# Adapter factors gathered per sequence and packed two to a pass, with weight rounding interleaved, in a one-core transformer block

## The chip, the cores and the metric

The kernel runs on one core of one Trainium2 chip. The metric is the device time of one execution, in microseconds, as the median of several runs. The profile comes from one further execution of the same program, taken by the hardware profiler.

## The reference

A batch `x` of 16 sequences of 128 tokens, 256 wide, in f32, goes through one block. A first attention conditions `x`; a gated delta-rule attention over it is added to `x`. What follows is the stage that the change is about:

```python
x = x + attn(cond(x, ...), ...)                     # call it x1
Ai, Bi = A[adapter_indices], B[adapter_indices]     # one of 8 adapters of rank 16 for each sequence
lora_linear(x, W, A, B) = x @ W + (x @ Ai) @ Bi
gate = lora_linear(x1, Wg, Ag, Bg)                  # 256 -> 1024
up   = lora_linear(x1, Wu, Au, Bu)
y    = lora_linear(silu(gate) * up, Wd, Ad, Bd)     # 1024 -> 256
qm(x, w, scale) = (x @ w.astype(float8_e4m3fn).astype(x.dtype)) * scale
x  = x1 + qm(silu(qm(y, gate_w)) * qm(y, up_w), down_w)     # 256 -> 768 -> 256
```

So each sequence needs only its own adapter, and the three weights of the last feed-forward part are first rounded to the values that an 8-bit float can hold.

## The kernel before, in words

The 16 sequences form four groups of four (`GS` = 4 sequences, `GT` = 512 tokens). The first two attentions take some 2040 us: 64 units (a key head and a group) go through a software pipeline whose steps have due times inside a slot; `plan` writes them down and a sort orders them. The scheduler of the language then settles the order of the instructions on each engine, and adds the waits. The last 420 us are the feed-forward stage, from line 875. Between the two, tiles of the new stage are placed over the memory of the old ones, so a first write there waits for whatever used that memory last.

**The seam.** `project` (L765) adds up each group's attention output in PSUM over the 16 units (L771). On the last unit VectorE adds `x` to it (L776) and SyncE's queue stores the result in the HBM buffer `x1` (L777). It does so in two halves; they share one buffer `x_in`, and the second half of `x` is loaded (L779, `load_x`) when the first half has been stored. `ffn_loads` (L787), called two slots after the last unit began, loads the adapters' first factors `ag`, `au`, the weights `wg`, `wu` and the second factors `bg`, `bu` into memory that the attention no longer uses.

**The feed-forward stage.** All of `x1` is loaded into `acc` (L886), then the other weights. The first and second factors of all 8 adapters stand side by side: 8 adapters x 16 ranks = 128 columns. The kernel computes all 128 ranks for every token and zeroes those of the other adapters: `onehot` (L908) has a one where a row belongs to a sequence's adapter, and `masked` (L928) multiplies with it on VectorE.

`adapted(g)` makes the steps of a group: two `turn`s (TensorE transposes, L941, and a ScalarE copy to `x1T`, L942), two `low`s (L947, one for gate and one for up), eight `hidden(i)`, then `low_down` (L969) and two `down`s (L978 and, for the adapter, L979). A `hidden` step computes 128 of the 1024 hidden columns: two matmuls with the weight (L955) and one with the second factor (L956) for the gate, SiLU on ScalarE (L962), the same three matmuls for up, and the product on VectorE (L964). `quantized(g)` is the 8-bit part: `fuse` (L997, L999, L1002, L1003) and `down` (L1011, VectorE's scale L1015, GpSimd's addition of `acc` L1016, the store L1017). `merge` interleaves the steps of `adapted(g)` with those of `quantized(g - 1)` evenly, by their place in their own lists; group 0's `adapted` runs alone.

**Rounding.** `quantize` (L911) rounds a weight in place. VectorE masks the exponent and scales it (L913, L914), adds and subtracts it (L915, L916); GpSimd checks for overflow in four instructions (L917 to L920). It is called for `gq`, `uq` and `dq` ahead of group 0's steps, and the three share one scratch buffer `qm`, so that each begins when GpSimd has finished the one before.

Of the kernel before, what the change touches and what calls it, by code (L numbers as in the profile page):

```python
# [8 lines left out]
F32 = mybir.dt.float32  # L9
# [6 lines left out]
P = 128  # L16
NB = 16
# [23 lines left out]
NAD = 8  # L41
QI = 768
# [11 lines left out]
def tile_adaln_attn_ffn(  # L54
# [4 lines left out]
    wg, wu, wd, ag, bg, au, bu, ad, bd,  # L59
# [47 lines left out]

    beta = keep.tile([P, NK, NB, 2], F32, name="beta")
# [6 lines left out]
    onehot = keep.tile([P, NB], F32, name="onehot")  # L115
# [267 lines left out]
    def load_o(u):  # L383
        kh, g = u
        wo = w_o[u] = late["w"].tile([P, 2, D], F32, name="wo_head", tag="wo")
        nc.sync.dma_start(out=wo, in_=w_out[kh * 2 * P : (kh + 1) * 2 * P, :].rearrange("(h p) e -> p h e", p=P))
        if kh == NK - 1:
            load_x(g, 0)

    def load_x(g, n):  # L390
        x_in[g, n] = late["p"].tile([P, 2, D], F32, name="x_in", tag="x_in")
        b0 = g * GS + 2 * n
        nc.sync.dma_start(out=x_in[g, n], in_=x[b0 : b0 + 2].rearrange("b s d -> s b d"))
# [359 lines left out]
    def finish_unit(u):  # L753

        kh, g = u
        d = un[u]

        def turn(n):
            ps = ps_b.tile([P, 4, S], F32, name="ps_zt", tag="b")
            for j in range(4):  # L760
                T.transpose(ps[:, j, :], d["z"][:, 4 * n + j, :], ident)  # L761
            d["zT", n] = late["p"].tile([P, 4, S], F32, name="zT", tag="zT", bufs=2)
            A.activation(d["zT", n], ps, AF.Copy, scale=nw)  # L763

        def project(n):  # L765
            if kh == 0:
                x_in[g, "ps", n] = ps_r.tile([P, 2, D], F32, name="ps_out", tag="r")
            ps = x_in[g, "ps", n]
            for j in range(2):
                for h in range(2):  # L770
                    T.matmul(ps[:, j, :], lhsT=d["zT", n][:, 2 * j + h, :], rhs=w_o[u][:, h, :],  # L771
                             start=kh == j == h == 0, stop=kh == NK - 1 and j == h == 1)
            if kh == NK - 1:
                part = x_in[g, n]
                b0 = g * GS + 2 * n
                V.tensor_tensor(part, ps, part, ALU.add)  # L776
                nc.sync.dma_start(out=x1[b0 : b0 + 2].rearrange("b s d -> s b d"), in_=part)  # L777
                if n == 0:
                    load_x(g, 1)  # L779
            if n == 1:  # L780
                del un[u]

        return [lambda: turn(0), lambda: turn(1), lambda: project(0), lambda: project(1)]
# [3 lines left out]
    def ffn_loads():  # L787
        def loaded(name, src, tag, **kw):
            t = pre[name] = pa.tile([P, FI], F32, name=name, tag=tag, **kw)
            nc.sync.dma_start(out=t, in_=src)  # L790

        low = pa.tile([P, 2, ND, P], F32, name="low_sb", tag="prod")
        for i, (name, src) in enumerate((("ag", ag), ("au", au))):
            pre[name] = low[:, i]
            nc.sync.dma_start(out=low[:, i], in_=src.rearrange("(c p) r -> p c r", p=P))
        loaded("wg0", wg[0:P], "kq", bufs=2)
        loaded("wg1", wg[P:D], "kq", bufs=2)
        loaded("bg", bg, "sqa")
        loaded("wu0", wu[0:P], "lanes")
        loaded("wu1", wu[P:D], "inv")  # L800
        loaded("bu", bu, "diag")
# [73 lines left out]
    with ExitStack() as st:  # L875
        w3 = st.enter_context(tc.tile_pool(name="w3", bufs=1))
        p3 = st.enter_context(tc.tile_pool(name="p3", bufs=2))
        ps_g = st.enter_context(tc.tile_pool(name="ps_g", bufs=4, space=PSUM))
        ps_x = st.enter_context(tc.tile_pool(name="ps_x", bufs=4, space=PSUM))
# [6 lines left out]
        acc = w3.tile([P, NB, D], F32, name="acc3", tag="acc3")  # L886
        for g in range(NG):
            nc.sync.dma_start(out=acc[:, g * GS : (g + 1) * GS, :], in_=x1[g * GS : (g + 1) * GS].rearrange("b s d -> s b d"))
        tok = loaded([P, NB], itok.partition_broadcast(P), "tok", I32)
# [3 lines left out]
        ad_sb = loaded([P, NFI, P], ad.rearrange("(c p) r -> p c r", p=P), "ad_sb")  # L893
        wd_sb = loaded([P, NFI, D], wd.rearrange("(c p) e -> p c e", p=P), "wd_sb")
        bd_sb = loaded([P, D], bd, "bd_sb")
# [5 lines left out]
        tokf = w3.tile([P, NB], F32, name="tokf")  # L901
        V.tensor_copy(tokf, tok)
        row_16 = w3.tile([P, 1], I32, name="row_16")
        G.iota(row_16, pattern=[[0, 1]], base=0, channel_multiplier=1)
        V.tensor_scalar(row_16, row_16, 4, None, ALU.arith_shift_right)
        rowf_16 = w3.tile([P, 1], F32, name="rowf_16")
        V.tensor_copy(rowf_16, row_16)
        V.tensor_scalar(onehot, tokf, rowf_16, None, ALU.is_equal)  # L908


        def quantize(t, n):  # L911
            m = w3.tile([P, QI * ND], F32, name="qm", tag="qm")[:, :n]
            V.tensor_scalar(m.bitcast(I32), t.bitcast(I32), 0x7F800000, None, ALU.bitwise_and)  # L913
            V.tensor_scalar(m, m, 2.0**-6, 1.5 * 2.0**20, ALU.max, ALU.mult)  # L914
            V.tensor_tensor(t, t, m, ALU.add)  # L915
            V.tensor_tensor(t, t, m, ALU.subtract)  # L916
            G.tensor_tensor(m, t, t, ALU.mult)  # L917
            G.tensor_scalar(m, m, 448.0 * 448.0, 3e38, ALU.is_gt, ALU.mult)
            G.tensor_scalar(m, m, 3e38, 0.0, ALU.mult, ALU.mult)
            G.tensor_tensor(t, t, m, ALU.add)  # L920

        quantize(gq.rearrange("p c f -> p (c f)"), ND * QI)
        quantize(uq.rearrange("p c f -> p (c f)"), ND * QI)
        quantize(dq.rearrange("p c e -> p (c e)"), NQI * D)
# [3 lines left out]
        def masked(dst, ps, g):  # L928
            V.tensor_tensor(dst.rearrange("p (s t) -> p s t", t=S), ps.rearrange("p (s t) -> p s t", t=S),
                            onehot[:, g * GS : (g + 1) * GS][:, :, None].to_broadcast([P, GS, S]), ALU.mult)  # L930

        def adapted(g):
            d = grp3[g] = {}

            def turn(c):
# [4 lines left out]
                for s in range(GS):  # L940
                    T.transpose(ps[:, s, :], acc[:, g * GS + s, c * P : (c + 1) * P], ident)  # L941
                A.copy(d["x"][:, c, :], ps.rearrange("p s t -> p (s t)"))  # L942

            def low(name, w):
                ps = ps_x.tile([P, GT], F32, name="ps_low", tag="x")
                for c in range(ND):
                    T.matmul(ps, lhsT=w[:, c, :], rhs=d["x"][:, c, :], start=c == 0, stop=c == ND - 1)  # L947
                d[name] = p3.tile([P, GT], F32, name=name, tag=name)
                masked(d[name], ps, g)

            def one_of(w, b, low_name, i):
                ps = ps_g.tile([P, GT], F32, name="ps_gu", tag="g")
                cols = slice(i * P, (i + 1) * P)
                for c in range(ND):
                    T.matmul(ps, lhsT=pre[f"{w}{c}"][:, cols], rhs=d["x"][:, c, :], start=c == 0, stop=False)  # L955
                T.matmul(ps, lhsT=b[:, cols], rhs=d[low_name], start=False, stop=True)  # L956
                return ps

            def hidden(i):
                pg = one_of("wg", pre["bg"], "lg", i)  # L960
                gs = p3.tile([P, GT], F32, name="gs", tag="gs")
                A.activation(gs, pg, AF.Silu)  # L962
                pu = one_of("wu", pre["bu"], "lu", i)
                V.tensor_tensor(d["h"][:, i, :], pu, gs, ALU.mult)  # L964

            def low_down():
                ps = ps_x.tile([P, GT], F32, name="ps_ld", tag="x")
                for i in range(NFI):
                    T.matmul(ps, lhsT=ad_sb[:, i, :], rhs=d["h"][:, i, :], start=i == 0, stop=i == NFI - 1)  # L969
                d["ld"] = p3.tile([P, GT], F32, name="ld", tag="ld")  # L970
                masked(d["ld"], ps, g)
                d["y"] = p3.tile([P, ND, GT], F32, name="yT", tag="yT")

            def down(e):
# [4 lines left out]
                T.matmul(ps, lhsT=bd_sb[:, cols], rhs=d["ld"], start=False, stop=True)  # L979
# [3 lines left out]
                [lambda: turn(0), lambda: turn(1), lambda: low("lg", pre["ag"]), lambda: low("lu", pre["au"])]  # L983
# [4 lines left out]
        def quantized(g):  # L988
# [17 lines left out]
            def down(n):  # L1006
# [9 lines left out]
                G.tensor_tensor(o, o, acc[:, b0 : b0 + 2, :], ALU.add)  # L1016
                nc.sync.dma_start(out=out[b0 : b0 + 2].rearrange("b s d -> s b d"), in_=o)  # L1017

            return [lambda i=i: fuse(i) for i in range(NQI)] + [lambda: down(0), lambda: down(1)]

        for g in range(NG + 1):
# [3 lines left out]
            if g:  # L1025
                lists.append(quantized(g - 1))
            merge(*lists)
# [8 lines left out]
def _layouts(i):  # L1036
# [4 lines left out]
    adapters = lambda a: c(np.asarray(a).transpose(1, 0, 2).reshape(a.shape[1], -1))  # L1041
    rows = lambda a: c(np.asarray(a).reshape(-1, a.shape[2]))
# [22 lines left out]
        "ag": adapters(i["L0_cond2_Ag"]),  # L1065
        "bg": rows(i["L0_cond2_Bg"]),
        "au": adapters(i["L0_cond2_Au"]),
        "bu": rows(i["L0_cond2_Bu"]),
        "ad": adapters(i["L0_cond2_Ad"]),
        "bd": rows(i["L0_cond2_Bd"]),  # L1070
# [23 lines left out]
```

## Time and profile before

| | us |
|---|---|
| median of 3 runs | 2471.11 (2468.83 to 2472.75) |
| the profiled execution's own time | 2466.78 |
| its span, first to last instruction | 2465.1 |
| last attention matmul L771 begins | 2039.05 |
| first matmul of the feed-forward stage begins | 2050.27 |
| product L964 that ended TensorE's longest wait in this stage begins | 2093.96 |
| L979 of group 0 begins | 2123.16 |
| last matmul L1011 begins its 10.52 us | 2449.03 |

How it is read: the page gives one execution on the slowest core, here the only one. The first part of the page is:

```profile
span 2465.1 us, 41929 instructions
PE 2233.8 (91%) x16264; PEld 1479.0 (60%) x16264; DVE 1548.6 (63%) x2099; ACT 1357.5 (55%) x3004; POOL 1123.0 (46%) x813
```

PE is TensorE's matmuls, PEld its weight loads, DVE VectorE, ACT ScalarE, POOL GpSimd. SP is SyncE, which here issues DMAs; "SPq" is its queue. The page's second part cuts the span into 40 equal slices of 61.6 us, with the busy share in tenths. In a timeline a row has the start, the length, the engine, the line, and out<-in with shapes; equal instructions that follow each other are merged, with x for their number, and in brackets stands how long the engine was idle ahead of the row and what ended that. A logical f32 matmul is two records. A row's length includes the time until the last result is out, so the distance between two starts is the better measure of what a row occupies.

### The profile page before, as it was taken

How to read it: one execution, taken by the hardware profiler on the slowest of the kernel's cores; microseconds unless marked ns; L12 is line 12 of the kernel's file. 1: busy time of each engine (PE TensorE's matmuls, PEld its weight loads, DVE VectorE, ACT ScalarE, POOL GpSimd, SP SyncE). 2: the span in 40 equal slices, each digit the busy share in tenths (PEclk: the TensorE clock that was granted, in tenths of full speed). 3: DMA queues.
4: the chain of work that ended last, by engine and by line, in shares of the span. 5: the costliest groups of instructions: out<-in, count | busy, mean ns of one | idle time of the engine just before them, and what ended most of it. 6: DMA issues, size and time to landing. Idle time of an engine off the chain costs nothing. (4 is left out here: it accounts for less than half of the span.)

```text
span 2465.1 us, 41929 instructions
## 1 busy us (share of the span) xinstructions
PE 2233.8 (91%) x16264; PEld 1479.0 (60%) x16264; DVE 1548.6 (63%) x2099; ACT 1357.5 (55%) x3004; POOL 1123.0 (46%) x813
## 2 busy tenths in 40 slices
PE   7868768999999899999989899998999996999999
PEld 3434336666767676676667666766767783444545
DVE  4657888777686967768696877769686523111111
ACT  4665546766767676667667666666766660111010
POOL 4685526555564656455564655556463214200000
PEclk9889879999999999999999999999999998999999
DMA  1200122222323222223223222233223213000000
GB/s 59 96 7 23 27 63 58 76 67 67 80 77 80 78 76 63 72 70 83 80 79 77 68 68 68 70 86 84 72 63 82 71 32 115 0 5 5 9 1 17
DMA packets 290580, 146.13 MB, mean 59 GB/s; under 512 B 184016, under 2 KB 279376, under 8 KB 290384
## 3 DMA queue, kind: packets, MB, share of 16 engines
q1 hardware_dynamic: 289952, 143.41, 21.5%
q8 instruction: 131, 2.15, 0.4%
q14 instruction: 65, 0.53, 0.1%
q10 hardware_dynamic: 432, 0.04, 0.0%
HBM read 116.91 MB, written 5.51 MB: 50 GB/s over the span
## 5 line engine op out<-in xcount | busy, mean ns | idle before, releaser
L437 DVE SCALAR_TENSOR_TENSOR cv<-ps_in,cw,cv 128x508 f32<-128x508 f32 (+2 forms) x768 | 541.1, 738 | 88.1 <-ACT cv L435 83.4
L426 PE MATMUL ps_in<-hT,w_v 128*128 128x512 f32 x512 | 280.7, 677 | 6.9 <-DVE z L741 4.6
L435 ACT ACTIVATE cv<-ps_in,cw 128x512 f32<-128x512 f32 x256 | 174.4, 681 | 187.3 <-PE ps_in L426 186.3
L741 DVE TENSOR_TENSOR z<-ps_ot,z 128x512 f32<-128x512 f32 x128 | 88.0, 687 | 290.5 <-ACT sq L739 290.5
L426 PE MATMUL ps_in<-hT,w_qk 128*128 128x512 f32 x512 | 248.9, 608 | 4.7 <-DVE z L741 3.5
L714 PE MATMUL ps_z<-w_gate,hT 128*128 128x256 f32 x1024 | 242.3, 379 | 1.7 <-DVE z L741 1.7
L771 PE MATMUL ps_out<-wo_head,zT 128*128 128x256 f32 x1024 | 238.8, 386 | 1.0 <-ACT zT L763 1.0
L771 PEld LDWEIGHTS ps_out<-wo_head,zT 128*128 128x128 f32 x1024 | 189.0, 190 | 38.0 <-issue 10.7
L471 POOL TENSOR_SCALAR nn<-turned 128x4 f32<-128x4 f32 x64 | 15.5, 242 | 428.8 <-DVE turned L466 326.5
L714 PEld LDWEIGHTS ps_z<-w_gate,hT 128*128 128x128 f32 x1024 | 189.8, 191 | 28.0 <-DVE z L741 2.6
L426 PEld LDWEIGHTS ps_in<-hT,w_v 128*128 128x128 f32 x512 | 103.2, 214 | 112.3 <-issue 104.3
L1016 POOL TENSOR_TENSOR o<-o,acc 128x512 f32<-128x512 f32 x8 | 10.1, 1264 | 341.9 <-DVE o L1015 341.9
L739 ACT ACTIVATE sq<-ps_ot 128x128 f32<-128x128 f32 x512 | 142.9, 279 | 31.9 <-PE ps_ot L733 23.1
L501 PEld LDWEIGHTS ps_kq<-kq 128*128 128x128 f32 x512 | 105.3, 208 | 75.9 <-issue 52.1
L727 ACT COPY y<-ps_y 128x512 f32<-128x512 f32 x128 | 74.9, 585 | 137.7 <-PE ps_y L726 136.5
L454 ACT ACTIVATE kq<-cv 128x512 f32<-128x512 f32 x128 | 80.1, 626 | 126.3 <-DVE cv L437 126.2
L748 POOL TENSOR_TENSOR z<-z,r 128x1024 f32<-128x1024 f32 x64 | 131.7, 2057 | 24.5 <-DVE z L741 21.8
L761 PE MATMUL ps_zt<-ident,z 128*128 128x128 f32 x512 | 88.0, 298 | 59.9 <-DVE aT L505 57.7
L426 PEld LDWEIGHTS ps_in<-hT,w_qk 128*128 128x128 f32 x512 | 93.6, 193 | 80.1 <-issue 64.9
L501 PE MATMUL ps_kq<-kq 128*128 128x256 f32 x512 | 140.7, 400 | 0.0
L733 PE MATMUL ps_ot<-y,aT 128*128 128x128 f32 x1024 | 135.3, 275 | 0.0
L726 PEld LDWEIGHTS ps_y<-v,W 128*128 128x128 f32 x1024 | 123.5, 194 | 16.5 <-ACT W L672 10.6
(205 smaller groups left out, 5051.3 us busy)
## 6 DMA issues: line engine op xcount, KB each, us to landing
aT<-sums SPq DMA_DIRECT2D x64, 512.0 KB, 5.5
w_qk<-in_w_qkv_dram SPq DMA_DIRECT2D x128, 128.0 KB, 2.3
w_v<-in_w_qkv_dram SPq DMA_DIRECT2D x64, 256.0 KB, 2.7
w_gate<-in_w_z_dram SPq DMA_DIRECT2D x64, 256.0 KB, 2.7
wo_head<-in_w_out_dram SPq DMA_DIRECT2D x64, 256.0 KB, 2.7
diag<-bT SPq DMA_DIRECT2D x256, 32.0 KB, 2.0
W<-Uc SPq DMA_DIRECT2D x256, 32.0 KB, 2.0
T<-Tc SPq DMA_DIRECT2D x128, 32.0 KB, 2.0
```

The source lines that it names most:

```text
L426: T.matmul(ps, lhsT=w[:, c, blk, :], rhs=hTs[g][:, c, :], start=c == 0, stop=c == ND - 1)
L435: A.activation(cv, psv, AF.Copy, scale=cw[:, col, 3:4])
L437: V.scalar_tensor_tensor(out=cv[:, :, sh:], in0=psv[:, :, : S - sh], scalar=cw[:, col, 3 - sh : 4 - sh], in1=cv[:, :, sh:], op0=ALU.mult, ...
L501: T.matmul(ps[:, j, :, :], lhsT=d["kq"][:, s, 0, :], rhs=d["kq"][:, s, :, :], start=True, stop=True)
L714: T.matmul(ps[:, j, :], lhsT=hTs[g][:, c, t0 : t0 + S], rhs=w_gate[u][:, c, :], start=c == 0, stop=c == ND - 1)
L726: T.matmul(ps[:, j, :], lhsT=d["W"][:, p, :], rhs=v[:, p, :], start=True, stop=True)
L733: T.matmul(ps[:, j, :], lhsT=d["aT"][:, p, :], rhs=d["y"][:, p, :], start=True, stop=True)
L739: A.activation(sq, ps[:, j, :], AF.Square, accum_out=d["r"][:, p : p + 1])
L741: V.tensor_tensor(z, ps, z, ALU.mult)
L748: G.tensor_tensor(d["z"], d["z"], d["r"][:, :, None].to_broadcast([P, NP, S]), ALU.mult)
L761: T.transpose(ps[:, j, :], d["z"][:, 4 * n + j, :], ident)
L771: T.matmul(ps[:, j, :], lhsT=d["zT", n][:, 2 * j + h, :], rhs=w_o[u][:, h, :], start=kh == j == h == 0, stop=kh == NK - 1 and j == h == 1)
```

## The change

- **Gathering.** The 16 adapter indices are loaded at the start, and some small VectorE and GpSimd instructions make row numbers of them (`rows_in`, `rows_out`). `adapter(g, ...)` has GpSimd issue five indirect DMAs a group: four fetch the first factors (gate, up and down of one adapter, 192 numbers on each of 128 partitions) of the group's sequences into `firsts`, one fetches the second factors (1280 numbers a partition). A ScalarE copy of 128x768 then puts the first factors in the order that the matmuls need. Group 0's are fetched in `ffn_loads`; those of the next groups are steps of their own in the merge (`next_adapter`). The tiles `adapters` of the later groups have two buffers, `firsts` one. The host lays the factors out as two tables.
- **64 ranks and halves.** A group has 4 sequences x 16 ranks = 64 ranks. One `low` computes gate (rows 0 to 63) and up (64 to 127) together: 2 matmuls instead of 4. In `hidden` the four weight matmuls come first, then two adapter matmuls, gate's on rows 0 to 63 and up's on rows 64 to 127 of TensorE. In `low_down` each matmul has 64 columns, even blocks into the lower half of PSUM's partitions and odd ones into the upper; the second factor of down is fetched twice, so that one 128-row matmul adds up the halves. The mask is the constant `fourth` (which sequence of the group a row belongs to) instead of `onehot`.
- **Rounding.** `quantize` returns three steps; the nine go into group 0's merge behind three empty ones, and VectorE's part of each is queued behind the latest product of `hidden` (`issue_after`).
- **x and x1.** In the last group the second half of `x` has a buffer of its own (one of `M2`'s) and is loaded along with the first. `x1` of group 0 is loaded in `ffn_loads`, and the others into one tile each, in place of `acc`.
- **PSUM.** The two pools of the stage change places.

```diff
-        for i, (name, src) in enumerate((("ag", ag), ("au", au))):
...
-        loaded("bg", bg, "sqa")
...
-        loaded("bu", bu, "diag")
+        adapter(0, pa.tile([P, GS * LA + LB], F32, name="adapters", tag="prod"),
+                pa.tile([P, GS * LA], F32, name="firsts", tag="sqa"))()
+        residual(0, pa.tile([P, GS, D], F32, name="x1_in", tag="diag"))
+
+    def adapter(g, t, raw):
+        for i in range(GS):
+            G.indirect_dma_start(raw[:, i * LA : (i + 1) * LA], None, low_in,
+                                 bass.IndirectOffsetOnAxis(rows_in[:, g * GS + i : g * GS + i + 1], 0))
+        G.indirect_dma_start(t[:, GS * LA :], None, low_out, bass.IndirectOffsetOnAxis(rows_out[:, g : g + 1], 0))
+        pre["a", g] = t[:, 0 : GS * LA].rearrange("p (q s r) -> p q s r", s=GS, r=R)
+        pre["b", g] = t[:, GS * LA :]
+        return lambda: A.copy(pre["a", g].rearrange("p q s r -> p s q r"), raw.rearrange("p (s q r) -> p s q r", s=GS, r=R))
...
-            def low(name, w):
+            def low():
                 ps = ps_x.tile([P, GT], F32, name="ps_low", tag="x")
                 for c in range(ND):
-                    T.matmul(ps, lhsT=w[:, c, :], rhs=d["x"][:, c, :], start=c == 0, stop=c == ND - 1)
+                    w = pre["a", g][:, 2 * c : 2 * c + 2].rearrange("p j s r -> p (j s r)")
+                    T.matmul(ps, lhsT=w, rhs=d["x"][:, c, :], start=c == 0, stop=c == ND - 1)
...
+                both = []
+                for w in ("wg", "wu"):
+                    ps = ps_g.tile([P, GT], F32, name="ps_gu", tag="g")
+                    for c in range(ND):
+                        T.matmul(ps, lhsT=pre[f"{w}{c}"][:, cols], rhs=d["x"][:, c, :], start=c == 0, stop=False)
+                    both.append(ps)
+                for ps, half in zip(both, HALVES):
+                    T.matmul(ps, lhsT=pre["b", g][half, cols], rhs=d["low"][half, :], start=False, stop=True)
...
                 for i in range(NFI):
-                    T.matmul(ps, lhsT=ad_sb[:, i, :], rhs=d["h"][:, i, :], start=i == 0, stop=i == NFI - 1)
+                    w = pre["a", g][:, 2 * ND + i].rearrange("p s r -> p (s r)")
+                    T.matmul(ps[HALVES[i % 2]], lhsT=w, rhs=d["h"][:, i, :], start=i < 2, stop=i >= NFI - 2)
...
+        def behind(f):
+            with tc.issue_after(grp3["product"].ins):
+                f()
...
-            if g:
+            if g == 0:
+                lists.append([lambda: None] * 3 + [lambda f=f: behind(f) for f in rounding])
+            else:
                 lists.append(quantized(g - 1))
+            if g + 1 < NG:
+                lists.append(next_adapter(g + 1))
```

## The prediction, on record ahead of the run

> **What bounds the kernel now.** I read the page first, then the stretches of the last 430 us, then TensorE's, VectorE's and GpSimd's timelines there. The page's slices put TensorE at 90% or more nearly everywhere. The two weak spots that the diff touches lie at the seam to the feed-forward stage, from 2042 us on:
>
> ```profile
> PE   7868768999999899999989899998999996999999
> POOL 4685526555564656455564655556463214200000
> ```
>
> ```profile
> 2045.00:2050.00 5.00, 0.00 (x0) 0.71 0.95 330
> 2050.00:2055.00 5.00, 4.73 (x13) 0.61 1.00 347
> ...
> 2085.00:2090.00 5.00, 0.81 (x2) 0.80 0.00 0
> 2090.00:2095.00 5.00, 0.31 (x1) 0.50 0.00 0
> 2095.00:2100.00 5.00, 5.00 (x9) 0.67 0.00 0
> 2100.00:2105.00 5.00, 5.00 (x13) 1.00 0.00 0
> ```
>
> These are length, TensorE's busy time, granted clock, DMA share, GB/s: two holes, each followed by a stretch at a lower clock. TensorE's timeline says what ended them:
>
> ```profile
> 2039.05 3.72 PE L771 MATMUL ps_out<-wo_head,zT 128*128 128x256 f32 x16 [0.34 <-ACT zT L763]
> 2050.27 1.97 PE L941 MATMUL ps_xt<-ident,acc 128*128 128x128 f32 x8 [7.50 <-DVE x_in L776]
> 2052.18 4.53 PE L947 MATMUL ps_low<-x1T,low_sb 128*128 128x512 f32 x8
> ...
> 2094.69 3.73 PE L955 MATMUL ps_gu<-x1T,wu 128*128 128x512 f32 x4 [8.88 <-DVE hid L964]
> ...
> 2109.43 7.03 PE L969 MATMUL ps_ld<-hid,ad_sb 128*128 128x512 f32 x16
> 2116.29 7.03 PE L978 MATMUL ps_y<-hid,wd_sb 128*128 128x512 f32 x16
> 2123.16 1.02 PE L979 MATMUL ps_y<-ld,bd_sb 128*128 128x512 f32 x2
> ```
>
> The first hole waits for the addition of x (its second half is loaded only when the first is stored), the second for a product queued on VectorE behind the rounding of a third weight, which itself waited for GpSimd:
>
> ```profile
> 2090.29 0.96 DVE L913 TENSOR_SCALAR qm<-dq 128x1536 int32<-128x1536 int32 x1 [12.83 <-POOL uq L920]
> ```
>
> After 2123 the matmuls follow each other without a hole up to 2459.55. A logical f32 matmul is two records; 16 records of L969 go from 2109.43 to 2116.29, so one 128x512 matmul costs 0.858 us and one with 256 columns 0.43. From the start of L979 (2123.16) to TensorE's end is 336.4 us; 5.55 us of result handling follow.
>
> **Matmuls of groups 1 to 3.** Ahead and after per group:
> - low: 4 matmuls become 2. Saves 1.72.
> - hidden, eight times: of 6 matmuls (5.15) the two adapter products become halves of TensorE's rows. The trace has such pairs, in the attention:
>
> ```profile
> 216.57 1.12 PE L426 MATMUL ps_in<-hT,w_qk 128*128 128x512 f32 x2
> 217.63 1.13 PE L217 MATMUL ps_sc<-ke,qT 64*128 64x512 f32 x4
> 218.69 0.66 PE L248 MATMUL ps_pt<-ident,sc 128*128 128x128 f32 x4
> ```
>
> Start to start, a full matmul ahead of a pair takes 1.06, and the pair of two takes 1.06 too: two at once for 0.86, and 0.20 for each change of shape. The Trainium skill (TensorEngine Tiling (Array Packing), Tiling Modes) says against this change that going from one tiling to another empties TensorE; these rows agree and give the price it lacks. So a hidden step is 4 x 0.858 + 0.20 + 0.858 + 0.20 = 4.69 and saves 0.46, not the 0.86 of free switching. Eight: 3.7 (6.9 without the price).
> - low_down: 8 matmuls of 64 columns in two column halves. The nearest row is L256, four 32-column blocks whose 8 records take 0.57 start to start, a single one's 0.43 and a switch: concurrency in columns is real. So 4 x 0.858 + 0.20 = 3.63 (0.14 more where it follows L1011) against 6.87: saves 3.1.
>
> That is 8.5 a group, 25.5 for three: L979's row to the end shrinks from 336.4 to 310.9. With free switching it would be 36.3. GpSimd's additions, stores and the end are unchanged. PSUM of a step is released 1.5 us after its end (0.60 and 0.69, rows L962 and L964, and 0.2), the next step lasts 3.4: no new wait.
>
> **The seam.** With x's second half loaded early and x1 of group 0 already in SBUF, the turns start at 2042.6 and end at 2043.5 (8 transposes, 0.88). But in the built program their first ScalarE copy, over reused SBUF, waits for the last store of x1. That one is issued at 2043.5 (VectorE's 0.69 after L771); the first store took from 2041.80 to 2045.88 with the same load traffic, the median is 2.4; I take 3.6, so 2047.1. Copies of 0.59: low runs from 2047.7 to 2049.4. TensorE has idled 4 us; before, 7.5 us of idling cost about 2 us of slow clock. I add 1.0 (0 to 2): 2050.4. Hidden steps 0 and 1 end at 2055.1 and 2059.8.
>
> **Rounding behind products.** VectorE's order is product 0, mask and scale gq, product 1, round gq; GpSimd then checks. Durations from before: 1.96 (L913, L914), 3.5 (L915, L916), 13.3 for GpSimd's four (2057.51 to 2070.82). They still form one chain through the single buffer qm. Product 1 is done at 2059.8 + 0.2 + 0.60 + 0.69, gq rounded at 2064.8; checked 2078.1; uq begun 2080.1, product 5 (0.69), uq rounded 2084.3; checked 2097.6; dq begun 2099.6, and its first addition 2101.4 (1.76). The mask of `ld` stands behind that addition on VectorE: 2102.1. TensorE meanwhile: six more hidden steps to 2088.0, low_down to 2091.6, the 8 products of down to 2098.5. There the adapter product that closes them waits for `ld`, and everything behind it on TensorE. So the hole of 8.88 goes, and one of 3.6 comes later, in group 0 alone; I add 0.8 of slow clock (0 to 1.8). The counterpart of L979 starts at 2102.9 instead of 2123.16: 20.3 gained. What packing saves inside hidden steps 2 to 7 of group 0 goes into this wait.
>
> **Gathers.** No indirect DMA is in the trace of before. Below stands an ordinary issue, 0.37 to 0.5 us on SP's queue; above, the skill (SBUF — State Buffer, A bandwidth-pool intuition that's wrong (but worth ruling out)) has a GpSimd-issued DMA go from about 620 to 3100 ns beside a VectorE copy. VectorE is nearly idle at the seam, so I take the 1 us that the skill gives for the GpSimd path's first byte (DMA: Bandwidth & Descriptors, Specifications) as an estimate of GpSimd's time p per gather, and 2.4 to landing (the store's median). No cost of a gather lies below zero. Groups 1, 2 and 3 take 4 gathers each, all ahead of gq's check on GpSimd, and each four wait for ScalarE's rearranging copy of the four before (one buffer; 0.9 us, from 0.585 for 512 elements); the fifth, of the second factors, fits into those waits. Two such copies also stand ahead of the first SiLU on ScalarE. With p = 1: the first four land at about 2046, copy to 2049.2, the next land at 2055.6, copy to 2056.5, SiLU 0 ends at 2057.1, hidden step 2 needs it at 2059.8: hidden. The last four end at 2060.5, ahead of 2064.8: hidden. From p = 1.2 on they show; beyond 1.6 GpSimd's check starts at 2039.6 + 12p + 6.6: p = 2 costs 5.5, p = 3 costs 17.5.
>
> Group 0's gathers stand near 1867 among GpSimd's factors (3 to 4 us; the product that needs them, L505, starts 6.8 us after they were ready) and are hidden for p under 1.7. Its copy is ahead of ScalarE's conv at 1925.71 and waits for the VectorE sum that ended at 1928.80: up to 3.9 us on ScalarE. TensorE has holes there and VectorE is late itself; I charge 0.3 (0 to 3). The index arithmetic at the start (12 small VectorE instructions, one DMA) ends well before VectorE's first mask at 24.88: nothing.
>
> **Sum.** 20.3 + 25.5 - 0.3 = 45.5. The profiled execution took 2466.78 (span 2465.1 and 1.7 around it): 2421.3. The median shown is 4.3 above it; carried over, 2471.1 - 45.5 = 2425.6.
>
> **Rivals.**
> - Switching is free: 36.3 instead of 25.5, 2414.8. Against it: the 1.06 rows. Chance 0.08.
> - The halves do not overlap, so the packing does not do what it says: each pair 1.72 + 0.40, low_down 6.87 + 0.2. Groups 1 to 3 lose 5 us, group 0 keeps some 14 from the seam and the chain is hidden: 2462. L217 speaks against it. 0.04.
> - Gathers of 2 to 3.5 us: the wait for `ld` grows to 9 to 26 us, 2431 to 2449. For it: their length is in no row. 0.13.
> - Slower: the same GpSimd queue at the seam, from p = 5.3 us (46.2 + 12p reaches 64.8 + 45.5). At 6 us the time is 2479. Only contention such as the 3.1 us above speaks for it. 0.03.
> - My forecast: 0.72, by itself 2418 to 2433.
>
> The range takes in free switching less a little on its low side, slow clocks, a charge of 3 us on ScalarE and gathers up to 2.6 us: 2413 to 2439; about 0.1 lies outside. A change within 0.2% (5 us) can't be told from none; only an in-between gather price (4.9 to 5.7 us) gives that.
>
> **What would show it.** Right: low's idle wait is ended by the copy of x1T, which waits for a store; a pair in hidden takes 1.06 start to start; TensorE's only long wait after 2060 is at the product of `ld` in group 0, ended by VectorE's mask, 2 to 6 us; groups 1 to 3 have no hole. Wrong: GpSimd's check starts well after gq is rounded (dear gathers); ScalarE's first SiLU ends after 2060; pairs of 0.86 or 1.9; new holes near 1925.

## The result, and the profile after

The changed kernel takes 2431.3 us (median of 4 runs, 2429.84 to 2432.56) beside 2470.5 for the kernel before on the same chip: ratio 0.9841 (95% interval 0.9824 to 0.9858), 39.2 us less. Predicted were 45.5 less, 2425.6 with a range of 2413 to 2439; 2431.3 lies 5.7 us above that figure and inside the range. The profiled execution took 2431.28, its span is 2429.6.

The stretches of the seam and of group 0 in the changed kernel, with the columns as before (length, TensorE's busy time and records, granted clock, DMA share, GB/s):

```profile
2050.00:2055.00 5.00, 1.42 (x2) 0.58 0.59 227
...
2110.00:2115.00 5.00, 4.07 (x5) 0.50 0.00 0
...
2125.00:2420.00 295.00, 295.00 (x836) 1.00 0.02 8
```

Two holes are left, each with a low clock in or behind it, and none from 2125 on. TensorE's timeline names what ended them (L800 is the old L771, L1018 the old L979):

```profile
2043.00 3.72 PE L800 MATMUL ps_out<-wo_head,zT 128*128 128x256 f32 x16 [0.34 <-ACT zT L792]
...
2053.58 3.78 PE L983 MATMUL ps_low<-x1T,adapters 128*128 128x512 f32 x4 [5.98 <-ACT x1T L977]
...
2110.93 2.07 PE L1018 MATMUL ps_y<-ld,adapters 128*128 128x512 f32 x2 [5.03 <-DVE ld L964]
2112.80 8.45 PE L1017 MATMUL ps_y<-hid,wd_sb 128*128 128x512 f32 x16
```

The second wait is for the mask of `ld`. On VectorE that mask stands behind the rounding of `dq`, which waited 9.92 us for GpSimd:

```profile
2106.53 0.96 DVE L941 TENSOR_SCALAR qm<-dq 128x1536 int32<-128x1536 int32 x1 [9.92 <-POOL uq L952]
...
2110.19 0.68 DVE L964 TENSOR_TENSOR ld<-ps_ld,fourth 128x512 f32<-128x512 f32 x1
```

Why was this chain late? ScalarE's timeline shows its start. The first SiLU (L999, at 2066.40) stands in ScalarE's queue behind the rearranging copy for group 2, and that copy waits for its gathers:

```profile
2052.94 1.07 ACT L977 COPY x1T<-ps_xt 128x512 f32<-128x512 f32 x2 [9.41 <-DMA gq<-in_gate_w_dram]
...
2065.66 0.83 ACT L837 COPY adapters<-firsts 128x768 f32<-128x768 f32 x1 [10.05 <-DMA firsts<-in_low_in_dram,rows_in]
2066.40 1.08 ACT L999 ACTIVATE gs<-ps_gu 128x512 f32<-128x512 f32 x2
```

And GpSimd's shows the gathers: 0.95 us each, 1.25 from start to start; the last one for group 2 is issued by 2060.59, and its data is there only at 2065.66:

```profile
2059.64 0.95 POOL L832 DMA_INDIRECT firsts<-in_low_in_dram,rows_in  x1 [0.31 <-issue]
...
2066.76 0.95 POOL L832 DMA_INDIRECT firsts<-in_low_in_dram,rows_in  x1 [4.93 <-ACT adapters L837]
```

The packed products do what was worked out. These rows stand at the end of group 0's hidden steps (L997 are the pairs on half of the rows, L1008 is `low_down`):

```profile
2089.43 1.13 PE L997 MATMUL ps_gu<-low,adapters 64*128 64x512 f32 x4
2090.49 1.98 PE L993 MATMUL ps_gu<-x1T,wg 128*128 128x512 f32 x4
...
2094.12 1.13 PE L997 MATMUL ps_gu<-low,adapters 64*128 64x512 f32 x4
2095.18 3.65 PE L1008 MATMUL ps_ld<-hid,adapters 128*64 128x512 f32 x16
2098.77 7.13 PE L1017 MATMUL ps_y<-hid,wd_sb 128*128 128x512 f32 x16
```

From start to start a pair takes 1.06 us, a whole step 4.69 (2089.43 to 2094.12) and `low_down` 3.59.

**A better ruler than the span.** L800 begins at 2043.00, the old L771 at 2039.05, though TensorE's instructions up to there are the same in the same order. All later readings are therefore taken from the start of that last attention projection. From it to the end of the span the kernel before takes 2465.1 - 2039.05 = 426.0 us, the changed one 2429.6 - 2043.0 = 386.6: 39.4 less, which agrees with the medians.

### The profile page after: what moved, and what is told of

Same layout as the page of the kernel before. It is cut to its first block, busy times and chain, and to the rows that moved or that the text cites. A ratio compares the mean times of both kernels' runs of the same rounds, so it can differ in the third digit from the quotient of the medians.

```text
span 2429.6 us, 41939 instructions
## 1 busy us (share of the span) xinstructions
PE 2200.7 (91%) x16248; PEld 1450.2 (60%) x16248; DVE 1548.1 (64%) x2102; ACT 1361.7 (56%) x3008; POOL 1145.9 (47%) x833
## 5 line engine op out<-in xcount | busy, mean ns | idle before, releaser
L466 DVE SCALAR_TENSOR_TENSOR cv<-ps_in,cw,cv 128x500 f32<-128x500 f32 (+2 forms) x768 | 540.2, 735 | 88.8 <-ACT cv L464 84.2
L800 PE MATMUL ps_out<-wo_head,zT 128*128 128x256 f32 x1024 | 238.8, 386 | 1.0 <-ACT zT L792 1.0
L800 PEld LDWEIGHTS ps_out<-wo_head,zT 128*128 128x128 f32 x1024 | 189.0, 190 | 38.0 <-issue 10.7
L1055 POOL TENSOR_TENSOR o<-o,x_in 128x512 f32<-128x512 f32 x8 | 10.1, 1265 | 283.4 <-DVE o L1054 283.4
```

Of the source, the lines that this page charges most:

```text
L466: V.scalar_tensor_tensor(out=cv[:, :, sh:], in0=psv[:, :, : S - sh], scalar=cw[:, col, 3 - sh : 4 - sh], in1=cv[:, :, sh:], op0=ALU.mult, ...
```

## The experiments

Theory: the time missing against the forecast is the wait for the mask of `ld`, which stands behind the chain of rounding and checks; ScalarE's queue makes that chain late. Rivals: the x1 store at the seam, TensorE's own path, the price of gathers and of shapes, a longer main stage. The "tail" is the span less the start of the last attention projection, "at ld" the start of L1018 of group 0 after that same point; each is worked out from one profile, and medians come from the timed runs. Beside the later kernels the kernel before took 2469.4 to 2470.1 us (medians), so their medians stand on one footing.

| kernel | median (runs) | projection begins | at ld | tail |
|---|---|---|---|---|
| before | 2470.5 (4) | 2039.1 | 84.1 | 426.0 |
| before_again | 2464.2 (1) | 2036.5 | 84.0 | 425.9 |
| changed | 2431.3 (4) | 2043.0 | 67.9 | 386.6 |
| after_again | 2432.9 (1) | 2043.3 | 68.6 | 387.8 |
| late_gathers | 2426.8 (5) | 2042.0 | 65.6 | 383.6 |
| own_x1T | 2430.0 (5) | 2041.6 | 68.4 | 386.7 |
| own_qm | 2428.1 (5) | 2045.3 | 65.6 | 381.9 |
| all_three | 2417.5 (5) | 2051.1 | 56.9 | 374.9 |
| mask_first | 2420.5 (5) | 2040.7 | 61.9 | 378.1 |
| all_four | 2415.2 (6) | 2041.0 | 55.1 | 371.3 |
| halves_apart | 2461.2 (12) | 2040.5 | 71.8 | 417.9 |
| columns_in_turn | 2431.4 (4) | 2040.8 | 66.9 | 388.5 |
| rounding_ahead | 2449.0 (4) | 2040.5 | 87.5 | 403.7 |
| late_x | 2436.1 (4) | 2042.6 | 73.5 | 391.2 |

### late_gathers

```diff
-            return [gather, lambda: d["arrange"]()]
+            if g == 1:
+                return [gather, lambda: d["arrange"]()]
+            return [lambda: None, lambda: behind(gather, "checked"), lambda: behind(lambda: d["arrange"](), "silu")]
```

(`behind` now takes the instruction to queue behind: "checked" is GpSimd's last check, "silu" ScalarE's latest SiLU.)

> Only the gathers of groups 2 and 3 are moved: GpSimd issues them behind its last check of dq, and ScalarE's rearranging copies stand behind a SiLU of the group before. Theory (ScalarE's first SiLU is stuck behind the copy of group 2, which waits for its gathers; with it gq's rounding, all of GpSimd's checks and the mask of ld): the first SiLU begins when the first pair ends, about 19 us after the last attention projection begins instead of 23.4; gq is rounded about 4.4 us earlier, the wait of TensorE at ld's product in group 0 falls from 5.0 us to about 0.7, and the slow clock behind it (2.3 us) mostly goes: 4.4 to 6.7 us less than the changed kernel, 2424.6 to 2427. Rival A (the late step is set by the x1 store that the x1T copy waits for): the wait at ld stays near 5 and the time within 1 us of 2431. Rival B (gathers are dear wherever they stand): new holes in groups 1 and 2 where they now run, time 2431 or more.

The first SiLU comes 18.9 us after the projection, as expected. But VectorE's and TensorE's rows show why only about half of these 4.5 us comes through:

```profile
2066.17 0.69 DVE L1000 TENSOR_TENSOR hid<-ps_gu,gs 128x512 f32<-128x512 f32 x1 [2.14 <-ACT gs L999]
2066.78 1.75 DVE L945 TENSOR_TENSOR gq<-gq,qm 128x1536 f32<-128x1536 f32 x1
```

```profile
2107.60 1.77 PE L1018 MATMUL ps_y<-ld,adapters 128*128 128x512 f32 x2 [3.30 <-DVE ld L964]
```

The second half of gq's rounding (L945, L946) is queued behind the second product, and that one now waits for TensorE's own pace. So gq is rounded 2.3 us earlier, and ld's product comes 2.3 us earlier; a low clock of 3.4 us remains behind its wait of 3.3. The tail is 3.0 us shorter (4.2 beside after_again), the median 4.5. The cause stands, its share in the end was put too high. Rival B has nothing for it: the gathers now run beside group 1's steps, from 2122.8 on, and TensorE has no hole there.

### own_x1T

```diff
-                    d["x"] = p3.tile([P, ND, GT], F32, name="x1T", tag="x1T")
+                    d["x"] = (keep.tile([P, ND, GT], F32, name="x1T", tag="hT", bufs=2) if g == 0 else
+                              p3.tile([P, ND, GT], F32, name="x1T", tag="x1T"))
```

> Only the x1T tile of group 0 gets memory that no x1 store reads (a free buffer of the hidden states). Theory (rounding chain ends group 0): the low product begins about 5 us after the last attention projection begins instead of 10.6, TensorE arrives at ld's product 6 to 8 us earlier, and waits there that much longer (11 to 13 us instead of 5.0), since GpSimd's check of gq still stands behind its own gathers of group 3, which wait for the copy of group 2: time within 1.5 us of 2431. Rival A (the store is what costs): 5 to 8 us less, 2423 to 2426.

TensorE's rows, and GpSimd's:

```profile
2046.45 1.98 PE L984 MATMUL ps_low<-x1T,adapters 128*128 128x512 f32 x4 [0.28 <-ACT x1T L978]
...
2110.00 2.08 PE L1019 MATMUL ps_y<-ld,adapters 128*128 128x512 f32 x2 [7.54 <-DVE ld L964]
```

```profile
2071.83 0.95 POOL L832 DMA_INDIRECT firsts<-in_low_in_dram,rows_in  x1 [0.30 <-issue]
2072.79 2.76 POOL L949 TENSOR_TENSOR qm<-gq 128x1536 f32<-128x1536 f32 x1
```

The low product starts 4.9 us after the projection (10.6 before), at full clock, and the tail does not change (386.7). Rival A falls: TensorE arrives earlier and waits longer, 7.5 us instead of 5.0. The expected 11 to 13 was too much, since TensorE also stops 4.3 us inside the hidden steps for the second SiLU, which here is the one behind the copy of group 2. The check of gq follows the last gather of group 3 with no gap. The run also corrects a label: the profile puts the wait of the x1T copy down to gq's load, but with that load untouched and only the memory changed it is gone. It was the x1 store; the profile of late_gathers, where this memory is as in the changed kernel, names that store for the same wait.

### own_qm

```diff
-            m = w3.tile([P, QI * ND], F32, name="qm", tag="qm")[:, :n]
+            m = w3.tile([P, QI * ND], F32, name="qm", tag="qm", bufs=3)[:, :n]
```

> Only the rounding's scratch gets three buffers, so that VectorE never waits for GpSimd's check of the projection before. Theory: the mask of ld no longer stands behind a waiting step, the 5.0 us wait at ld's product goes (under 0.7 us), and the slow clock after it (2.3 us) as well; TensorE's arrival there is unchanged. 5 to 7.4 us less: 2424 to 2426. Rival (the wait only moves: GpSimd's third check ends later than the quantized stage needs it, or the low clock stays because of the earlier hole): a hole of several us at the first quantized products, 2428 to 2431.

The wait shrinks to 2.4 us, and there is no low clock behind it; the tail is 4.7 us shorter. The median lies at the edge of what the rival gives, but the rival's hole at the first quantized products is not there. Why is the wait not zero? VectorE's rows, and those of GpSimd at the same time:

```profile
2099.07 4.14 DVE L941 TENSOR_SCALAR qm<-dq 128x1536 int32<-128x1536 int32 x1
2103.24 2.10 DVE L942 TENSOR_SCALAR qm<-qm 128x1536 f32<-128x1536 f32 x1
2105.38 4.86 DVE L945 TENSOR_TENSOR dq<-dq,qm 128x1536 f32<-128x1536 f32 x1
```

```profile
2097.02 5.38 POOL L950 TENSOR_SCALAR qm<-qm 128x1536 f32<-128x1536 f32 x1
2102.48 2.05 POOL L951 TENSOR_SCALAR qm<-qm 128x1536 f32<-128x1536 f32 x1
2104.61 4.01 POOL L952 TENSOR_TENSOR uq<-uq,qm 128x1536 f32<-128x1536 f32 x1
```

The same three VectorE instructions take 0.96, 0.96 and 1.76 when GpSimd is idle (the changed kernel). Here each ends 0.8 to 1.6 us after the GpSimd instruction that it met (2103.21 after 2102.40, 2105.34 after 2104.53, 2110.24 after 2108.62): it stands still while that one runs, and then does its own work. Two of GpSimd's are longer as well: L951 and L952 take 2.05 and 4.01, where the changed kernel has 1.47 and 3.42. This agrees with the Trainium skill (SBUF — State Buffer, Who interferes with whom), which calls the port that the two share an exclusive lock, not a split of bandwidth. The single scratch buffer had kept the two engines apart.

### all_three

The three edits together.

> Late gathers, own x1T and three scratch buffers together. Theory: no wait over 1 us is left between the last attention projection and the quantized products of group 0; ld's product starts about 55 us after the last attention projection begins (67.9 in the changed kernel), the low product at full clock. About 13 us plus 2.3 us of slow clock: 2416 (2414 to 2420). Rival (TensorE's path is held elsewhere, by gq's load or by VectorE's rounding between products): holes in the hidden steps, 2421 to 2426, no better than the best of the three alone.

ld's product starts at 56.9 (55 expected), and one wait over 1 us is left there, 2.1 us for the mask, for the cause just seen.
The tail is 11.7 us shorter, the median 13.8. That is more than the three give one by one (tails 3.0, nothing and 4.7): an earlier start of TensorE is worth nothing as long as the mask comes last, as own_x1T showed, and counts once the mask is early.

### mask_first

```diff
-                lists.append([lambda: None] * 3 + [lambda f=f: behind(f) for f in rounding])
+                lists.append([lambda: None] * 3 + [lambda f=f: behind(f) for f in rounding[:6]] + [lambda: None] * 3)
+                lists.append([lambda: None] * 17 + [lambda f=f: behind(f, "mask") for f in rounding[6:]])
```

> Only the three dq steps of the rounding move: VectorE has them behind the mask of ld of group 0 and not ahead of it. Theory (the wait at ld's product is the place in VectorE's queue behind a step that waits for GpSimd, not TensorE's own path): the wait of 5.0 us is gone (0 to 0.5), the slow clock after it (2.3 us) too, with ld's product about 63 us after the last attention projection begins instead of 67.9. 5 to 7.4 us less: 2424 to 2426.5. Rival (the wait is owed to the checks as such, and only moves to the first quantized products): those products start less than 3 us earlier, 2428 to 2431.

```profile
2095.63 7.13 PE L1017 MATMUL ps_y<-hid,wd_sb 128*128 128x512 f32 x16
2102.60 1.02 PE L1018 MATMUL ps_y<-ld,adapters 128*128 128x512 f32 x2
```

VectorE's rows show the new order:

```profile
2095.77 0.69 DVE L964 TENSOR_TENSOR ld<-ps_ld,fourth 128x512 f32<-128x512 f32 x1 [2.31 <-PE ps_ld L1008]
2103.37 0.96 DVE L941 TENSOR_SCALAR qm<-dq 128x1536 int32<-128x1536 int32 x1 [6.90 <-POOL uq L952]
```

There is no wait at ld and no low clock behind it, and the quantized products follow on time. The tail is 8.5 us shorter, with the late SiLU and the store untouched. Of this 5.0 are the wait and 2.4 the clock (from L1018 to the first quantized product it is 9.0 us here and 11.4 in the changed kernel). The last 1.0 is not the edit's: the low product happens to start 9.6 us after the projection here and 10.6 there. The rival falls: the checks were not needed that early, only the mask was. The median, 2420.5, is better than expected; this profile's main stage ended 2.3 us earlier than the changed kernel's, which the edit does not touch.

### all_four

The three of all_three and the new order of mask_first.

> Late gathers, own x1T, three scratch buffers, and the dq steps behind the mask of ld. Theory: the last wait of 2.1 us at ld's product and its 3.4 us of slow clock go: 2.1 plus about 1.5 us less than the first three together, 2414 (2412 to 2415.5), the shortest of all, with ld's product 54.8 us after the last attention projection begins. Rival (with VectorE's steps now running beside GpSimd's checks, both slow each other): a hole at the first quantized products, 2416 or more.

2415.2 us: ratio to the kernel before 0.9774 (0.9751 to 0.9797), 16 us less than the changed kernel. The tail of 371.3 is the shortest; TensorE's longest wait up to ld's product is 0.33 us, and that product starts at 55.1, where 54.8 was expected.

### halves_apart

```diff
-                for ps, half in zip(both, HALVES):
-                    T.matmul(ps, lhsT=pre["b", g][half, cols], rhs=d["low"][half, :], start=False, stop=True)
+                    half = HALVES[w == "wu"]
+                    T.matmul(ps, lhsT=pre["b", g][half, cols], rhs=d["low"][half, :], start=False, stop=True)
```

(The new lines stand inside the loop over the two projections.)

> The two second factors of a hidden step keep their half of the rows, but each stands right behind its own projection's products, so that the two never run side by side and the shape changes four times a step instead of twice. Theory (0.20 us per change of shape, 0.86 us for a product of half the rows alone): a step takes 8 x 0.43 + 2 x 0.86 + 4 x 0.20 = 5.96 us start to start instead of 4.69, that is 30.5 us over the 24 steps of groups 1 to 3, and about 5 more in group 0, whose 10 us are half hidden by the wait at ld: 2462 to 2468. Rival (no price for a change, only the overlap counts): 5.16 us a step, 11 us plus nothing in group 0: 2441 to 2443.

```profile
2060.21 1.98 PE L993 MATMUL ps_gu<-x1T,wg 128*128 128x512 f32 x4
2062.13 1.12 PE L996 MATMUL ps_gu<-low,adapters 64*128 64x512 f32 x2
...
2066.15 1.98 PE L993 MATMUL ps_gu<-x1T,wg 128*128 128x512 f32 x4
```

A step takes 5.94 us start to start, where 5.96 was worked out. In group 0 TensorE now arrives too late to wait for the mask. So 0.20 us per change of shape holds, and pairs side by side are what makes the half rows pay: apart, a step is longer than the 5.15 of the kernel before. The median is 0.8 us below the expected span.

### columns_in_turn

```diff
-                for i in range(NFI):
+                for i in (0, 2, 4, 6, 1, 3, 5, 7):
```

(in `low_down`; the even blocks go to the lower half, the odd ones to the upper)

> The eight products of the down adapter's first factor are ordered half by half (0, 2, 4, 6, then 1, 3, 5, 7) and no longer alternate between the two halves of the columns; the same instructions otherwise. Theory (neighbours on different halves run side by side): the group of products takes about 6.9 us instead of 3.65, 3.2 us more in each of groups 1 to 3, and nothing in group 0, where the wait at ld shrinks by as much: 2441 (2440 to 2442.5). Rival (a product of 64 columns is short by itself, whatever stands beside it): 2431.

```profile
2091.90 5.42 PE L1008 MATMUL ps_ld<-hid,adapters 128*64 128x512 f32 x16
2097.25 7.13 PE L1017 MATMUL ps_y<-hid,wd_sb 128*128 128x512 f32 x16
```

A miss for both: the 16 records take 5.35 us start to start, neither 6.9 nor 3.6. So 64 columns in one half cost 0.67 us a product, 0.45 when halves alternate, 0.86 with all columns (prediction). Of the saving in low_down about half comes from the alternation. Why one half alone is already shorter, no run here settles. The median is that of the changed kernel, as the rival said, but not for its reason. Three groups lose 3 x 1.8 = 5.3 us, and group 0 pays 3.4 of it back: ld's product starts 1.0 us earlier and the 2.4 of low clock stay away. The tail is 1.9 us longer, as this sum gives.

### rounding_ahead

```diff
-                lists.append([lambda: None] * 3 + [lambda f=f: behind(f) for f in rounding])
+                for f in rounding:
+                    f()
```

> Only the place of the rounding is undone: VectorE's steps are traced ahead of group 0 again and not queued behind its products. Theory (products would stand behind steps that wait for GpSimd's checks, which themselves stand behind GpSimd's gathers): two holes in the hidden steps of group 0, ld's product about 87 us after the last attention projection begins instead of 67.9, the slow clock moved and not gone: 17 to 21 us more, 2448 to 2452. Rival (GpSimd's chain ends at the same time either way, so the place costs nothing): 2431.

```profile
2089.77 3.78 PE L993 MATMUL ps_gu<-x1T,wu 128*128 128x512 f32 x4 [9.55 <-DVE hid L1000]
...
2106.96 3.78 PE L993 MATMUL ps_gu<-x1T,wu 128*128 128x512 f32 x4 [4.63 <-DVE hid L1000]
```

GpSimd's rows show why the products wait:

```profile
2069.26 0.94 POOL L832 DMA_INDIRECT firsts<-in_low_in_dram,rows_in  x1 [0.30 <-issue]
2070.21 2.77 POOL L949 TENSOR_TENSOR qm<-gq 128x1536 f32<-128x1536 f32 x1
```

As expected, 2449.0 with ld's product at 87.5: the queueing is worth 17.7 us of this change (17.1 by the tails). The gathers on GpSimd hold its checks back: that of gq begins 29.7 us after the projection, right behind the last gather, though gq is rounded at 17.9; in the kernel before it began at 18.5.

### late_x

```diff
-        kw = dict(tag="M2", bufs=2) if g == NG - 1 and n else dict(tag="x_in")
+        kw = dict(tag="x_in")
```

(and the second load back behind the first store)

> Only the early load of the last half of x is undone: it comes again into the first half's memory, after that half's sum has been stored. Theory: the last x1 store, the x1T copy behind it and the low product come 5 to 6 us later (about 16 us after the last attention projection begins instead of 10.6), but GpSimd's chain, which waits for the copy of group 2 anyway, only 1.5 to 2 us later: 2 to 4 us more, 2433 to 2435. Rival A (TensorE's path sets the end of group 0): 6 us more, 2437. Rival B (the gathers decide alone): 2431.

The low product starts at 18.8 (16 expected), the first SiLU 4.1 us later than in the changed kernel (2 expected), the median is 4.8 us longer, between my figure and rival A's. TensorE's path alone still does not set the end: it waits 3.3 us at ld for the mask. The transfers were under-estimated again: the last store was issued at 2054.82, and the load that waits for it at 2060.36. The early load is worth 3.5 to 4.8 us (by the tails, beside after_again or the changed kernel, and by the medians).

### before_again and after_again

> The kernel before once more, unchanged. Theory (the start of the last attention projection varies by several us from execution to execution with the windows in which TensorE's clock is low in the first 420 us, and the change has no part in it): that start lies anywhere between 2039 and 2047, other than 2039.05, with other low windows in the first 420 us, and the stretch from there to the end is again 426.0 within 0.5. Rival (the change made the main stage 3.95 us longer): it starts within 0.5 us of 2039.05.

> The changed kernel once more, unchanged. Theory: the start of the last attention projection is not 2043.0 again but anywhere between 2039 and 2047; from there to the end 386.6 within 1 us. Rival (the change made the main stage longer): within 0.5 us of 2043.0.

The unchanged kernel before begins its last projection at 2036.5 this time, below the 2039 to 2047 that I expected, the changed one at 2043.3. The tail of the kernel before repeats to 0.1 us, the changed one's to 1.2; tails that differ by less say nothing. In all 12 profiles with the changed kernel's main stage that start lies between 2040.5 and 2051.1. The low clock is one thing that differs between the two executions of the kernel before, first the one already shown, then this one:

```profile
70.00:80.00 10.00, 9.46 (x30) 0.54 0.01 2
```

```profile
70.00:80.00 10.00, 8.56 (x43) 1.00 0.01 2
```

The same work meets the low clock at other moments (0.54 and 1.00 from 70 to 80 us, 1.00 and 0.83 from 90 to 100). But the second execution is 2.2 us ahead already at 55 us, where the clock over the first 60 us is 0.94 in both; what moves the start is not isolated by any run. The second expectation was half missed: 2043.3 is next to 2043.0.

Did the change make the main stage longer? Both profiles of the kernel before are of quick executions (2466.8 and 2464.2 us, medians 2469.4 to 2470.5), so their early starts are no measure. With its tail of 426.0 and the 1.7 us around the span, the execution of 2470.5 us starts the last projection at about 2042.8; the changed kernel's of 2431.3 does so at 2043.0 (2041.8 with the tail of after_again). Within about 1 us the main stage is the same.

## Why the prediction was right, and where its terms were off

- **Groups 1 to 3: right.** Predicted 25.5. From L1018 (L979) of group 0 to the end the kernel before takes 426.0 - 84.1 = 341.9 us, the changed one 386.6 - 67.9 = 318.7; with the 2.4 us of low clock behind the wait taken out, 25.6 are saved. A pair takes 1.06 and a step 4.69, as worked out; low_down 3.59 for 3.63. The other 13.8 of the 39.4 come from the seam and group 0.
- **The kind of the remaining wait: right.** TensorE stops once in group 0, at ld's product, for VectorE's mask. From the last projection to there the prediction has 84.1 - 20.3 = 63.8 us including 0.8 for the clock; measured are 67.9 and then 2.4 of low clock. That the wait itself is so close (5.0 us, predicted 3.6) is partly luck: TensorE arrived 3.4 us later after the projection than worked out (62.9 instead of 59.5) and the mask was ready 4.8 later.
- **The step that failed is that of the gathers:** "the next land at 2055.6, copy to 2056.5, SiLU 0 ends at 2057.1, hidden step 2 needs it at 2059.8: hidden". Even with the 3.95 us by which that execution was later, this puts the landing at 2059.6; it was 2065.7, 6.1 later. The first SiLU ended at 2067.0, 2063.0 without the 3.95: a sign of being wrong that the prediction names (after 2060) came true. The price on GpSimd was 1.25 us each (1 assumed, and 1.2 named as the limit), which makes 1.0 of the 6.1. The mis-sized term is the landing, 2.4 us assumed and 6.2 and 5.1 measured (2048.63 to 2054.78; 2060.59 to 2065.66), twice in a row because of the single `firsts` buffer. The prediction took a median for it, though it quotes 4.1 us for a store beside the same loads. gq was rounded 30.6 us after the projection instead of 25.8, and all behind it by the same 4.9. late_gathers shows the cause, and that with the SiLU on time about half of this would still have been left.
- **The rival of dear gathers** (2 to 3.5 us each, 2431 to 2449) has the measured time at its edge, but it is not what happened: a gather costs GpSimd 1.25, and the check of gq begins at 2073.72, 0.1 us after gq is rounded.
- **The seam's store** was mis-sized the same way: 3.6 us assumed, 5.3 measured (2047.5 to 2052.8), and the low clock took 2 us, not 1. Neither reached the end, as own_x1T shows.
- **The clock behind the wait:** 0.8 assumed, 2.4 measured. These 1.6 and the 4.9 make 6.5; groups 1 to 3 give 0.1 back. Missing in the tail are 45.8 - 39.4 = 6.4 (45.8 is the forecast without the 0.3 near 1925).
- **ScalarE's copy near 1925:** charged 0.3, nothing seen. ScalarE's next instruction did come 3.9 us late (1933.63, against 1925.71 and a lag of 4.07), but the lag between the two executions, 4.07 us at 1917, is 3.94 at 1946.
- **What I took for given:** that the chain of rounding had to be paid. One change of order, mask_first, takes 7.4 us of wait and low clock out with nothing else.

## What to carry to other kernels

When a small instruction that others wait for (a mask, a SiLU) is queued on its engine behind one that waits for a DMA or for another engine, order it first before making the chain shorter: here that gave 7.4 us, more than each repair of the chain alone (3.0 to 4.7, and nothing). Cost a gather by issue and landing, and take the landing from transfers beside the same loads, not from a quiet median. Compare executions from a common late instruction, because what happens in an earlier stage can move everything by more than the effect sought: by 2.5 us between the two executions of the kernel before.

## What was not expected of the hardware

- VectorE's rounding instructions beside GpSimd's: 3.7 to 4.9 us instead of 0.96 and 1.76, in own_qm and all_three.
- Gathers issued by GpSimd: 0.95 us and 0.30 to the next, 1.4 to 2.2 beside VectorE's rounding (a smaller slowdown than the one that the prediction quotes), and 5 to 6 us to landing beside weight loads.
- Products of 64 columns: 0.67 us in one half, 0.45 alternating, 0.86 for 128.
- A low clock of 6.8 us came with the waits at ld of 5.0 and 7.5 us, one of 3.4 us with those of 3.3 (late_gathers, late_x) and 2.1 (all_three), and none with those of 2.4 (own_qm) and 3.3 (columns_in_turn): its length is not a function of the wait alone.
